# A graph layer on one core: rows turned in the table's loop, words read in the selection, and one run in 12 fetched by SyncE

## The chip, the cores and the metric

The kernel runs on one core of one Trainium2 chip. A core has TensorE (PE), VectorE (DVE), ScalarE (ACT), GpSimd (POOL) and SyncE (SP); each works through its own instructions in their order, and semaphores tie them together. SP computes nothing here: it only issues transfers. The metric is the time of one execution on the device in microseconds. The kernel before takes 3628.49 us (the median of three runs, 3622.15 to 3631.22).

## The reference

A graph has N = 12500 nodes of 128 floats (32 scalars and 32 vectors of three) and E = 412500 edges, sorted by the node that they point to. Cut to what matters:

```python
f0, f1 = x0 @ W1_0e, einsum(x1, W1_1o)          # node features; one half goes along the edges, one stays
e0, e1 = feat0[edge_src], feat1[edge_src]       # one row of 128 floats gathered for every edge
h = gelu(gelu(edge_scalar_attr @ W_mlp1) @ W_mlp2)
w00, w01, w10, w11 = h @ Wp_00, h @ Wp_01, h @ Wp_10, h @ Wp_11     # 4 x 32 weights of an edge
mid = products of w.. with e0, e1 and the edge's four attributes
n0, n1 = segment_sum(mid0, edge_dst), segment_sum(mid1, edge_dst)
y = cos(pi/8) * self + sin(pi/8) * (n @ W2)
out = layernorm(x + y)
```

## The kernel before

**Runs and chunks.** The edges are cut into 806 runs of 512 (four columns q = 0..3 of 128 edges), and four runs make a chunk `c`. For each run `s` a tile `G[s]` (128 partitions, 4 columns, 128 floats) receives the feature row of every edge's source node. There are `LEAD` = 19 such tiles, so run s + 19 takes the tile of run s.

**Four ways to fill a column of G.** All features are first computed into a `table` in device memory.
- POOL gathers a column with an indirect DMA (`gather`, L220), one for each 128 edges. This is the usual way.
- DVE and ACT fill one column of some runs from `xT`, the node matrix kept turned in SBUF: they load node numbers into registers (L176), copy one column of `xT` for each edge (`pick`, L188 and L190), and PE and ACT turn the 128 copies into rows of G (`picked_rows`, L196 and L197). 184 runs get column 2 and 157 runs get column 1 in this way.
- SP fills column 3 of the runs in `aided`, from run 36 on one run in `AID` = 14: 55 runs. `aid(s, t)` loads 16 row numbers into registers (L203) and issues 16 transfers of one row of 512 bytes (L207); eight such groups make a column. The groups of run a are spread over the 12 iterations from a - 16: at the iterations a - 16, -15, -13, -12, -10, -9, -7 and -6. POOL leaves out the columns filled otherwise.
- The first 18 runs (`raw_runs`) are gathered before the table exists: POOL gathers their rows from the input x, PE transposes them (`turn_rows`, L569), ACT copies them to a tile `xt` (L571), PE multiplies by the weights (`features`, L577), and ACT writes the result to a tile `ft` (L579), which then stands for `G[s]`.

**The two loops.** Order on PE, ACT, DVE and SP is the order of the program text (`manual_schedule`); POOL has little but gathers. The table's loop (L875 to L887, iterations b = 0 to 26) loads blocks of 512 nodes, turns them into `xT`, multiplies, and stores the features; small jobs stand at given b (`extra`). The main loop (L907 on) has one iteration for each run s. In it PE makes the edge weights of the coming runs (`weights`, L560), sums the messages of run s - 1 (`segments`, L631 and L633), and DVE makes the messages of run s (`messages`, L602 and twice L606) from the weights in PSUM and from G, with groups of picks in between. `select(c + 1)`, at the end of a chunk, makes the selection matrices of the next chunk (L587 and L595).

**What stands in SP's queue.** In each iteration's order: the edge scalars of four chunks on (`load_edges`, one in four iterations, L487), now and then indices and attributes (L471, L504), the groups of `aid`, and, in `normalise`, the stores of finished nodes (L257), which wait until DVE and ACT have normalised them. A tile is given out again when all its readers are done; an instruction that has to wait for more semaphores than it holds gets instructions ahead of it in the queue that only wait (EVENT_SEMAPHORE).

Of the kernel before, what the change touches and what calls it, by code (L numbers as in the profile page):

```python
# [8 lines left out]
F32 = mybir.dt.float32  # L9
# [12 lines left out]
P = 128  # L22
# [3 lines left out]
Q = 4  # L26
SB = P * Q
J = 8
CH = 4
# [12 lines left out]
LEAD = 19  # L42
RAW = 18
MARGIN = 64
ACC = 768
AID = 14
ROWS = 16
AID_FROM = 36
AID_LEAD = 16
# [2 lines left out]
COL_Q = {DVE: Q - 2, ACT: Q - 3}  # L52
COL_FROM = {DVE: 12, ACT: 16}
LNB = 2


@with_exitstack
def gnn_kernel(ctx: ExitStack, tc: tile.TileContext, x, src, dst, ea4, ea8, w1_0, w1_1, wm1, wm2,
# [8 lines left out]
    nc = tc.nc  # L67
# [55 lines left out]
    for e in SLOTS:  # L123
        picked[e] = []
        while True:
# [3 lines left out]
                break  # L129
            picked[e].append(at + 2)  # L130
    pick_of = {(e, s): i for e, g in picked.items() for i, s in enumerate(g)}
    assert AID_FROM >= raw_runs and AID_LEAD < LEAD and P % ROWS == 0 and STEPS <= AID
    assert all(raw_runs <= g[0] and 0 < len(g) <= 3 * P for g in picked.values())
    assert 0 < len(aided) <= P
# [430 lines left out]
    def turn_rows(s):  # L565

        pt = ps.tile([P, Q, P], F32, name="h")
        for q in range(Q):
            nc.tensor.transpose(pt[:, q, :], G[s][:, q, :], ident)  # L569
        XR[s] = wk.tile([P, Q, P], F32, name="xt", bufs=3)  # L570
        nc.scalar.activation(XR[s], pt, AF.Copy)  # L571

    def features(s):

        pf = ps.tile([P, Q, P], F32, name="h")
        for q in range(Q):
            nc.tensor.matmul(pf[:, q, :], XR[s][:, q, :], wf, start=True, stop=True)  # L577
        G[s] = wk.tile([P, Q, P], F32, name="ft", bufs=3)
        nc.scalar.activation(G[s], pf, AF.Copy)  # L579

    def select(c):


        n = min(CH, NS - c * CH)
        b, r = divmod(c * CH, P)
        oh = wk.tile([P, CH, Q, J], F32, name="oh", bufs=1)
        nc.vector.tensor_tensor(oh[:, :n], iota[:, None, None, :J].to_broadcast([P, n, Q, J]),  # L587
                                rel[b][:, :, r:r + n].rearrange("p q s -> p s q")[:, :, :, None]
                                .to_broadcast([P, n, Q, J]), op=OP.is_equal)
        hot = oh[:, :n].rearrange("p s q j -> p (s q) j")  # L590
        t0 = c * CH % ET * Q
        a = e4[c * CH // ET][:, :, t0:t0 + n * Q].rearrange("p k t -> p t k")
        S_own[c] = owns[c % 2]
        to = S_own[c].rearrange("p t (k j) -> p t k j", j=WIDE)[:, :n * Q, :4, :J]
        nc.vector.tensor_tensor(to, hot[:, :, None, :].to_broadcast([P, n * Q, 4, J]),  # L595
                                a[:, :, :, None].to_broadcast([P, n * Q, 4, J]), op=OP.mult)
# [259 lines left out]
    with tc.manual_schedule(engines={PE, ACT, DVE, SP}):  # L856
        load_raw_rows(nc.sync, 0, min(3, raw_runs))
        load_w1(nc.scalar)
        if raw_runs > 3:
            load_raw_rows(nc.scalar, 3, raw_runs)  # L860
        for s in range(min(LEAD - 2, raw_runs)):
            gather(s)
        nc.vector.tensor_scalar(ident, diag, 0.0, None, op0=OP.is_equal)
        for b in range(min(3, NG)):
            XT[b] = load_nodes(b)
        make_wf()
        clear()
        loads = list(weight_loads())
        new_sums()
        extra = {2: lambda: load_edges(0), 3: lambda: load_attributes(0), NG // 2 - 2: lambda: turn_attributes(0), 4: lambda: load_raws(0), NG // 2: lambda: load_indices(0),  # L870
                 NG // 2 + 3: make_w1b, NG // 2 + 5: make_ws, NG - 6: lambda: radial(0), NG - 4: lambda: mlp1(0),
                 NG - 2: lambda: mlp2(0), NG - 1: make_wpost,
                 NG // 2 + 1: lambda: nc.vector.memset(A["next"], 0.0),
                 NG - 3: tile_places}
        for b in range(NG + 2):  # L875
            if b < NG:
                turn(b)
            if 0 < b <= NG:
                features_of(b - 1)
            if 1 < b:  # L880
                store_nodes(nc.scalar, table, b - 2, PF[b - 2])
            if b + 3 < NG:
                XT[b + 3] = load_nodes(b + 3)
            if b > 4 and loads:
                nc.sync.dma_start(*loads.pop(0))
            if b in extra:
                extra[b]()  # L887
        assert not loads
        for c in range(1, min(EDGES_AHEAD, NCH)):
            load_edges(c)  # L890
        if aided:
            aid_load()
        for s in range(min(LEAD - 2, raw_runs), min(LEAD - 1, NS)):
            gather(s)
        if NCH > 1:
            radial(1)
            mlp1(1)
            mlp2(1)
        weights(0, range(Q))
        select(0)  # L900
        for s in range(min(2, raw_runs)):
            turn_rows(s)
            features(s)
        A["now"] = A["next"]
        clearing = []
        pick_nodes(ACT, 0, 0)
        for s in range(NCH * CH + CH):  # L907
            c, k = divmod(s, CH)
            if s + LEAD - 1 < NS:
                gather(s + LEAD - 1)  # L910
            if k == 3 and c + EDGES_AHEAD < NCH:
                load_edges(c + EDGES_AHEAD)
            if s % P == P // 2 - 16 and (s // P + 1) * P < NS:
                load_raws(s // P + 1)
            if s % P == P // 2 and (s // P + 1) * P < NS:
                load_indices(s // P + 1)
            if s % ET == 8 and s - 8 + ET < NS:
                load_attributes(s // ET + 1)
            for t in range(P // ROWS):
                a = s + AID_LEAD - t * STEPS // (P // ROWS)  # L920
                if a in aided:
                    aid(a, t)
            end = c == NCH - 1
            if k % 2 == 0:
                pick(ACT, len(picking[ACT]) // 2)
            if k % 2 == 0 and s + 2 < NS:
                weights(s + 2, range(Q // 2))
            if k % 2 == 1 and s + 1 < NS:
                weights(s + 1, range(Q // 2, Q))
            if 0 < s <= NS:  # L930
                segments(s - 1)
            if k == 0 and c < NCH:
                places(c)
            if k == 0 and c + 2 < NCH:
                radial(c + 2)
            if s % ET == 21 and s - 21 + ET < NS:
                turn_attributes(s // ET + 1)
            for e in picked:
                if (e, s + 2) in pick_of:
                    picked_rows(e, pick_of[e, s + 2])  # L940
            if k > 1 and c + 2 < NCH:
                pick(ACT, P)
                (mlp1 if k == 2 else mlp2)(c + 2)
                if k == 3 and c + 3 == NCH:
                    nc.scalar.activation(spent, ones, AF.Sqrt)
            pick(ACT, P)
            pick_nodes(ACT, s + 1, 0)
            if s + 2 < raw_runs:
                turn_rows(s + 2)
            if s < NS:  # L950
                for part in range(3):
                    messages(s, part)
                    pick_nodes(DVE, s, part)
                    pick(DVE, P)
            if s + 2 < raw_runs:
                features(s + 2)
            if k == (1 if end else 2) and 0 < c <= NCH:
                add(c - 1)
            if k == 1 and clearing and c < NCH:
                clear_sums(clearing.pop(0)[1])  # L960
            if k < 3 and s < NS:
                pick_nodes(DVE, s, 3)
                pick(DVE, P)
            if k == 1 and 1 < c < NCH:
                norm_on(due.get(c - 2, []))
            if k == 2 and 1 < c < NCH:
                norm_end(due.get(c - 2, []))
            if k == 0 and c == NCH:
                norm_on(due.get(c - 2, []))
                norm_end(due.get(c - 2, []))  # L970
            if c == NCH and k == 1:
                norm_last(due[c - 1])
            if k == (1 if end else 3) and 0 < c < NCH:
                norm(due.get(c - 1, []))
                clearing += [(c, a) for a in range(4)] if c - 1 in due and c < NCH else []
            if k == 3 and c + 1 < NCH:
                select(c + 1)
            if k == 3 and s < NS:
                pick_nodes(DVE, s, 3)
                pick(DVE, P)  # L980
            if s == 1:
                addresses()
                find_first()
                new_sums()
                clearing = [(0, a) for a in range(4)]
            if s == NS - 8:
                count_odd()
# [31 lines left out]
```

## Time and profile before

| | |
|---|---|
| median of three runs | 3628.49 us |
| the profiled execution, its own time | 3639.84 us |
| its span, first to last instruction | 3637.6 us |
| granted TensorE clock, mean | 0.932 |
| busy: PE, DVE, POOL, ACT | 3236.3, 3069.3, 2690.1, 2598.0 us |
| POOL's gathers from the table | 2755 |
| SP's single-row transfers | 7040 |
| messages of the first and last run start at | 102.9 and 3616.9 us |

A row of a group names the line, the engine, the operation and the tiles written and read, then how often it came and how long it took. An engine's name with a q behind it (SPq, DVEq) is its queue: instructions there are not counted as busy time, so SP has no row among the engines. A row of waits says which queue or engine stood at which line until what had ended, with the sum in us, the number of times and the longest. In a row of windows each engine has its busy time and, in brackets, its instructions.

### The profile page before, as it was taken

The page shows a single profiled execution, that of the slowest core. Times are in us where ns is not written, and L with a number is a line of the kernel's source. Part 1 is how long each engine was busy: PE and PEld are TensorE (multiplying, and loading weights), DVE is VectorE, ACT ScalarE, POOL GpSimd, SP SyncE. Part 2 cuts the span into 40 slices and gives each one's busy share as a digit, 9 for nine tenths or more (in the row PEclk, how much of TensorE's full clock was granted, in tenths as well). Part 3 has the DMA queues.
Part 4 walks back from the last instruction along what each step waited for, and adds up shares of the span by engine and source line. Part 5 has one row for each costly group of instructions (what it writes and reads, how often), then busy time and mean ns, then how long its engine had stood idle before and what let it go on. Part 6 is the DMA issues. An engine that isn't in the chain of part 4 may idle for free.

```text
span 3637.6 us, 139391 instructions
## 1 busy us (share of the span) xinstructions
PE 3236.3 (89%) x28542; PEld 2792.6 (77%) x28542; DVE 3069.3 (84%) x27134; ACT 2598.0 (71%) x21720; POOL 2690.1 (74%) x2833
## 2 busy tenths in 40 slices
PE   5899899999889999899889899899989889889998
PEld 4677777787777777777778777788777777777777
DVE  4388888888888888888888888888888888888886
ACT  2377777777777777677767777677777777777785
POOL 7667777777777777777777777777777777777773
PEclk8999998989899999799989999989989999999999
DMA  8223323223322323322223332232232323232231
GB/s 205 54 51 70 63 59 68 63 59 74 63 59 61 69 60 68 68 59 62 65 62 64 70 64 62 58 69 63 65 69 63 61 67 63 62 68 60 63 66 30
DMA packets 579923, 240.84 MB, mean 66 GB/s; under 512 B 484075, under 2 KB 529014, under 8 KB 579078
## 3 DMA queue, kind: packets, MB, share of 16 engines
q0 software_dynamic: 90464, 185.45, 20.0%
q1 hardware_dynamic: 467844, 39.94, 9.0%
q10 hardware_dynamic: 20770, 6.47, 0.8%
q8 instruction: 252, 4.13, 0.5%
q14 instruction: 593, 4.86, 0.4%
HBM read 218.82 MB, written 12.80 MB: 64 GB/s over the span
## 4 chain that ended last, share of the span: by engine, by line
DVE 46%; PE 13%; issue 11%; ACT 7%; DVEq 7%; SPq 7%; POOL 5%; DMA 4%; ACTq 0%; POOLq 0%
DVE gt L188 25%; DVE M L606 13%; DVEq L176 7%; SPq L207 5%; POOL G L220 5%; ACT gt L190 5%; PE sums L631 3%; PE sums L633 3%; DVE own L595 2%; DMA G<-table,idx 2%; DVE M L602 2%; PE w L560 2%; DVE acc L646 2%; PE h L665 2%; SPq L203 1%
## 5 line engine op out<-in xcount | busy, mean ns | idle before, releaser
L220 POOL DMA_INDIRECT G<-table,idx x2755 | 2620.8, 951 | 869.4 <-issue 743.1
L190 ACT ACTIVATE gt<-xT 128x1 f32 x20096 | 1972.2, 189 | 246.1 <-issue 244.4
L188 DVE COPY gt<-xT 128x1 f32 x23552 | 1709.3, 145 | 315.2 <-issue 287.1
L631 PE MATMUL sums<-own,M 128*128 128x96 f32 x6446 | 1348.8, 292 | 5.8 <-DVE M L606 5.5
L633 PE MATMUL sums<-own,M 128*128 128x96 f32 x6446 | 1307.0, 286 | 43.7 <-DVE M L606 43.5
L631 PEld LDWEIGHTS sums<-own,M 128*128 128x128 f32 x6446 | 1039.4, 201 | 101.2 <-DVE M L606 20.5
L633 PEld LDWEIGHTS sums<-own,M 128*128 128x128 f32 x6446 | 1030.0, 201 | 59.6 <-DVE M L606 58.8
L606 DVE TENSOR_TENSOR M<-w,G 128x384 f32<-128x384 f32 x1576 | 861.8, 547 | 0.2
L560 PE MATMUL w<-wpb,h 64*128 64x128 f32 x6448 | 698.3, 308 | 118.4 <-DVE M L606 117.6
L560 PEld LDWEIGHTS w<-wpb,h 64*128 64x128 f32 x6448 | 528.0, 199 | 277.4 <-DVE M L606 150.5
L602 DVE TENSOR_TENSOR M<-w,G 128x256 f32<-128x256 f32 x788 | 328.5, 417 | 35.8 <-PE w L560 8.9
L527 PE MATMUL h<-eT,w1b 64*128 64x128 f32 x3232 | 296.2, 311 | 64.1 <-ACT G L197 54.0
L527 PEld LDWEIGHTS h<-eT,w1b 64*128 64x128 f32 x3232 | 244.6, 209 | 97.2 <-ACT G L197 63.1
L542 PE MATMUL h<-h,w2b 64*64 64x256 f32 x3232 | 282.6, 409 | 31.8 <-ACT h L531 26.4
L197 ACT ACTIVATE G<-h 128x128 f32<-128x128 f32 x341 | 91.2, 272 | 289.7 <-PE h L196 244.2
L531 ACT ACTIVATE h<-h 128x512 f32<-128x512 f32 x404 | 216.0, 585 | 82.0 <-PE h L527 78.4
L547 ACT ACTIVATE h<-h 128x512 f32<-128x512 f32 x404 | 214.3, 580 | 35.5 <-PE h L542 29.6
L542 PEld LDWEIGHTS h<-h,w2b 64*64 64x64 f32 x3232 | 128.6, 138 | 113.4 <-ACT h L531 41.4
L196 PE MATMUL h<-wf,gt 128*128 128x128 f32 x682 | 143.2, 300 | 9.1 <-ACT h L531 5.1
L595 DVE TENSOR_TENSOR own<-oh,e 128x512 f32<-128x512 f32 x202 | 139.8, 692 | 7.1
L646 DVE TENSOR_TENSOR acc<-sums,acc 128x384 f32 x202 | 111.2, 551 | 19.4 <-issue 14.2
L520 ACT ACTIVATE eT<-h 128x128 f32<-128x128 f32 x202 | 53.9, 267 | 97.8 <-PE h L518 77.7
(112 smaller groups left out, 1294.1 us busy)
## 6 DMA issues: line engine op xcount, KB each, us to landing
G<-table SPq DMA_DIRECT2D x7040, 0.5 KB
G<-table,idx POOLq DMA_INDIRECT x2755
e<-in_edge_attr SPq DMA_DIRECT2D x201, 64.0 KB
xt<-in_x SPq DMA_DIRECT2D x24, 256.0 KB
table<-ft ACTq DMA_DIRECT2D x24, 256.0 KB
xt<-in_edge_attr SPq DMA_DIRECT2D x24, 256.0 KB
out<-y SPq DMA_DIRECT2D x24, 256.0 KB
xt<-in_dst SPq DMA_DIRECT2D x5, 256.0 KB
```

Source lines behind the costliest of these rows:

```text
L176: _, r = nc.values_load_multi_w_load_instructions(pick_rows[e, i][:, r0:r1], engines=[e], min_val=x_at, max_val=x_at + 4 * (N - 1), skip_r ...
L188: nc.vector.tensor_copy(to, col)
L190: nc.scalar.activation(to, col, AF.Copy)
L220: nc.gpsimd.indirect_dma_start(out=G[s][:, q, :], out_offset=None, in_=x if s < raw_runs else table, in_offset=bass.IndirectOffsetOnAxis(a ...
L527: nc.tensor.matmul(p1[h][:, j // 2, j % 2, :], w1b[rows, j, :], eT[c][rows, :], start=True, stop=True)
L531: nc.scalar.activation(H1[c][h], p1[h].rearrange("p k j e -> p (k j e)"), AF.Gelu_apprx_tanh, scale=1.0 / math.sqrt(RAD))
L542: nc.tensor.matmul(p2[r][k * HID:(k + 1) * HID, h * n:(h + 1) * n], w2b[rows, :], H1[c][h][rows, k * n:(k + 1) * n], start=True, stop=True)
L560: nc.tensor.matmul(WP[i][:, q, :], H2[c][q % 2][rows, k, q // 2, :], wpb[rows, :], start=True, stop=True)
L602: nc.vector.tensor_tensor(M[s][:, :, :, :MUL], w[:, :, :2 * MUL].rearrange("p q (a u) -> p q a u", a=2), g[:, :, None, :MUL].to_broadcast( ...
L606: nc.vector.tensor_tensor(M[s][:, :, j, MUL:].rearrange("p q (i u) -> p q i u", i=3), w[:, :, None, (2 + j) * MUL:(3 + j) * MUL].to_broadc ...
L631: nc.tensor.matmul(flat[:, bass.ds(at, 4 * FIRST_HALF)].bitcast(F32), M[s][:, q, 0, :], own[:, 3 * WIDE:], start=False, stop=False)
L633: nc.tensor.matmul(sb[:, 1:, bass.ds(at, 4 * WIDE)].bitcast(F32), M[s][:, q, 1, :], own[:, :3 * WIDE].rearrange("p (a j) -> p a j", a=3), ...
```

## The change

Three things are done at once.

- `AID` goes from 14 to 12: the runs whose column 3 comes from SP are 36, 48, ..., 804, which are 65 in place of 55. SP issues 8320 rows in place of 7040; POOL makes 10 gathers fewer. The iterations at which the eight groups of one run are issued, counted from the run, stay as they are.
- `turn_rows` and `features` of the first 14 runs move from the main loop (and from the place just ahead of it) into the table's loop: run i is turned at iteration `TURN_AT[i]` and multiplied one iteration later. The turned rows go into a tile of the ring `M`, and the features are written back into `G[s]`; the tiles `xt` and `ft` are no longer used for this. Runs 14 to 17 stay in the main loop at iterations 12 to 15.
- `select(c)` gets small copies on DVE between L587 and L595, for chunks 10 to 199: one word of each gathered column of the last two runs of that chunk, and one word of each row that SP fetched for an aided run of that chunk. They go into a tile `SEEN` that nothing reads. A copy waits until the transfers that fill what it reads have landed; each engine's queue remembers which counts it has seen.

```diff
-AID = 14
+AID = 12
+TURN_AT = (5, 7, 9, 11, 12, 14, 15, 16, 17, 18, 20, 21, 23, 24)
...
     def turn_rows(s):
...
-        XR[s] = wk.tile([P, Q, P], F32, name="xt", bufs=3)
+        XR[s] = wk.tile([P, Q, 2, P], F32, name="M", bufs=3)[:, :, 0, :]
         nc.scalar.activation(XR[s], pt, AF.Copy)
...
     def features(s):
...
-        G[s] = wk.tile([P, Q, P], F32, name="ft", bufs=3)
+        XR.pop(s)
         nc.scalar.activation(G[s], pf, AF.Copy)
+
+    SEEN = cst.tile([P, 4 * Q], F32)
+    seen_at = [0]
+
+    def read(rows):
+
+        i = seen_at[0] % (4 * Q)
+        seen_at[0] += Q
+        nc.vector.tensor_copy(SEEN[:, i:i + rows.shape[1]], rows)
+
+    def seen(s):
+
+        got = [q for q in range(Q) if not (q == Q - 1 and s in aided or any(q == COL_Q[e] and (e, s) in pick_of for e in picked))]
+        while got:
+            step = got[1] - got[0] if len(got) > 1 else 1
+            n = 1
+            while n < len(got) and got[n] == got[0] + n * step:
+                n += 1
+            read(G[s][:, got[0]:got[n - 1] + 1:step, 0])
+            got = got[n:]
...
     def select(c):
...
         hot = oh[:, :n].rearrange("p s q j -> p (s q) j")
+        if raw_runs <= c * CH - LEAD and (c + 2) * CH < NS:
+            for s in range((c + 1) * CH - 1, (c + 1) * CH - 3, -1):
+                seen(s)
+            for s in range(c * CH, (c + 1) * CH):
+                if s in aided:
+                    read(G[s][:, Q - 1:, 0])
...
             if b in extra:
                 extra[b]()
+            if XR:
+                features(next(iter(XR)))
+            if b in TURN_AT:
+                turn_rows(TURN_AT.index(b))
...
         select(0)
-        for s in range(min(2, raw_runs)):
-            turn_rows(s)
-            features(s)
+        if XR:
+            features(next(iter(XR)))
+        early = len(TURN_AT)
...
-            if s + 2 < raw_runs:
+            if early <= s + 2 < raw_runs:
                 turn_rows(s + 2)
...
-            if s + 2 < raw_runs:
+            if early <= s + 2 < raw_runs:
                 features(s + 2)
```

More of the change, by code (lines that the diff above doesn't have):

```diff
@@ L131, in gnn_kernel @@
     pick_of = {(e, s): i for e, g in picked.items() for i, s in enumerate(g)}
+    assert len(TURN_AT) <= raw_runs <= LEAD - 1 and TURN_AT[-1] < NG + 2
     assert AID_FROM >= raw_runs and AID_LEAD < LEAD and P % ROWS == 0 and STEPS <= AID
```

## The prediction

> **What bounds the kernel now.** First the page: the span, the busy shares, and the groups of POOL and DVE.
>
> ```profile
> span 3637.6 us, 139391 instructions
> PE 3236.3 (89%) x28542; PEld 2792.6 (77%) x28542; DVE 3069.3 (84%) x27134; ACT 2598.0 (71%) x21720; POOL 2690.1 (74%) x2833
> ...
> L220 POOL DMA_INDIRECT G<-table,idx x2755 | 2620.8, 951 | 869.4 <-issue 743.1
> ...
> L188 DVE COPY gt<-xT 128x1 f32 x23552 | 1709.3, 145 | 315.2 <-issue 287.1
> ```
>
> No engine is full by its share. POOL's 74% deceives, though: its idle time is "issue", a fixed pause behind each gather. The view of windows gives its real pace (header, then a stretch in the middle), and the source views of the gather and of the messages (L602, L606) say how far it is ahead.
>
> ```profile
> core 0: us, PE busy (x) PEld busy (x) DVE busy (x) ACT busy (x) POOL busy (x), PEclk, DMA share, GB/s
> 2000.00:3000.00 1000.00, 895.99 (x7945) 774.04 (x7942) 871.22 (x7840) 742.54 (x6287) 756.95 (x798) 0.94 0.30 65
> ...
> L220 POOL DMA_INDIRECT G<-table,idx x2755: 938/944/1467, 94.3 to 3583.3; - x197
> ...
> L602 DVEq EVENT_SEMAPHORE  x1894: 21/50/1855, 109.2 to 3615.1; - x190
> L602 DVE TENSOR_TENSOR M<-w,G x788: 351/415/426, 203.6 to 3616.9; 128x256 f32<-128x256 f32 x197
> L602 DVE TENSOR_TENSOR M<-w,ft x18: 401/425/426, 102.9 to 199.6; 128x256 f32<-128x256 f32 x18
> ...
> L606 DVE TENSOR_TENSOR M<-w,G x1576: 535/547/558, 204.7 to 3617.7; 128x384 f32<-128x384 f32 x197
> ```
>
> 798 gathers in 1000 us are 1.253 us each, so 2755 take 3452 us: POOL has no pause to give away. The messages go at (3616.9 - 203.6) / 787 = 4.34 us for a run, and the last gather starts 33.6 us, or 7 to 8 runs, ahead of the last message. So PE and DVE, in their written order, set the pace, with POOL close behind.
>
> The third queue is in no row of busy time. SP's source views (L207, L203), and two pieces of its timeline:
>
> ```profile
> L207 SPq MOVE G<-table x7040: 29/29/103, 155.2 to 3561.8; - x196
> L207 SPq DMA_DIRECT2D G<-table x7040: 227/228/544, 196.5 to 3561.9; - x196
> ...
> L203 SPq TENSOR_LOAD <-aid_at x440: 1160/1262/1804, 153.7 to 3555.2; - x147
> ```
> ```profile
> 1925.44 18.66 SPq L207 DMA_DIRECT2D G<-table  x48
> 1944.20 0.41 SPq L487 DMA_DIRECT2D e<-in_edge_attr  x1
> 1946.06 18.26 SPq L207 DMA_DIRECT2D G<-table  x48
> ...
> 2038.15 5.11 SPq L207 DMA_DIRECT2D G<-table  x16
> 2061.54 1.95 SPq L257 DMA_DIRECT2D out<-y  x2
> ```
>
> Three groups of 16 rows and one transfer of edge scalars take 1946.06 - 1925.44 = 20.62 us with no pause between them. Only ahead of the stores at 2061.54 does SP stand still, for some 18 us. How much it stands still in all, from its first row to its last, is in the view of SP's waits for 196 to 3563 us:
>
> ```profile
> SPq L257 <- ACT y L704: 191.9, 21, 21.4
> SPq L207 <- DVE M L606: 57.6, 18, 8.7
> SPq L207 <- PE h L569: 41.2, 1, 41.2
> SPq L257 <- ACT G L197: 20.8, 2, 19.6
> SPq L207 <- DMA xt<-in_src: 3.6, 2, 3.2
> ```
>
> The 41.2 us end with the first row. In the 3365 us from 196.5 to 3561.9 SP therefore waits some 270 us (191.9 + 57.6 + 20.8), 8%, for stores and for free G tiles, and works 3095 us. This 8% is all that it can take on.
>
> **The change part by part.**
>
> *AID from 14 to 12.* SP gets 10 runs more, each 8 loads of row numbers and 128 rows. What a run costs, in two ways. From the timeline: 20.62 us less 0.5 for the edge scalars (0.41 and its wait) over three groups is 6.71 us, times 8 is 53.7 us. From the stage: 3095 us less all else in SP's queue, over 55. All else is, by its source views (L487, L257, L504),
>
> ```profile
> L487 SPq DMA_DIRECT2D e<-in_edge_attr x202: 368/405/2088, 11.9 to 3562.8; - x101
> ...
> L257 SPq DMA_DIRECT2D out<-y x25: 384/411/889, 334.1 to 3632.8; - x25
> ...
> L504 SPq DMA_DIRECT2D xt<-in_edge_attr x25: 347/372/1779, 136.8 to 3505.6; - x25
> ```
>
> 227 transfers at 0.5 us with the wait beside each, and L504 with a dozen loads of indices at 0.45: 130 us. That leaves 2965 / 55 = 53.9 us. SP's work becomes 65 x 53.7 + 130 = 3620 to 65 x 53.9 + 130 = 3634 us; I take 3625. The stage began with 3365 us, waits and all, so SP no longer fits: 12 runs at 4.34 us are 52.1 us, and in them SP has one aided run and three edge transfers, 53.9 + 1.5 = 55.4 us. It falls behind by over 3 us in 12 runs; its waits vanish first, then DVE waits for it. Behind the late rows in SP's queue stand the edge scalars (PE's `radial` waits), the stores, and indices.
>
> How late may SP be? The last group of run a is issued at iteration a - 6; the new copy in `select` asks for it at a - 1 (36 and 12 are multiples of 4, so an aided run opens its chunk). Edge scalars loaded at iteration 4c + 3 are used at 4c + 8. So after five iterations, some 22 us, the other engines go at SP's pace of 55.4 / 12 = 4.62 us a run.
>
> The Trainium skill, DMA: Bandwidth & Descriptors, section "Issuing engines are not separate DMA queues", says that issuing from another engine only saves sequencer time, "which is usually small relative to the DMA itself". By that rule ten more fetched runs would cost SP next to nothing, and the second case below would be the result (3551 us instead of 3828). The trace does not agree here: for a row of 512 bytes the issue, 228 ns and a move beside it, is what fills SP.
>
> POOL loses 10 gathers, 12.5 us by 1.253 us; hidden, since POOL is then not the last.
>
> *Words read in the selection.* Per chunk about three copies of a few words, and one more in a third of the chunks; the nearest row is L188's copy of one word, 0.145 us: 0.5 us a chunk, 0.12 us a run, with a few waits of 50 ns. In return the waits ahead of L602 go (1894 x 50 ns = 95 us, 0.12 us a run) and some of the 287.1 us that L188 stands idle behind them. The bounds of the net are a loss of 0.12 and a gain of 0.12 + 287.1 / 788 = 0.48 us a run; I take a gain of 0.1, because two waits in the queue are the usual and only the pause behind them can shrink. The copies ask for gathers four runs early; POOL is 7 to 18 runs ahead, so they hold nothing up: `own` (L595), the picks and PE's `segments` stand behind them. As long as SP is last, all of this is cover work and worth nothing.
>
> *Fourteen runs turned in the table's loop.* What a turned run costs PE, and what room there is (page groups, then windows of the first 100 us with the columns above):
>
> ```profile
> L577 PE MATMUL h<-wf,xt 128*128 128x128 f32 x144 | 20.8, 288 | 13.8 <-ACT xt L571 13.8
> L569 PE MATMUL h<-ident,G 128*128 128x128 f32 x72 | 11.8, 288 | 5.5 <-ACT h L547 2.8 <-ACT h L531 2.7
> ```
> ```profile
> 0.00:50.00 50.00, 29.72 (x187) 27.92 (x188) 21.35 (x34) 10.73 (x17) 35.61 (x44) 0.86 0.97 221
> 50.00:100.00 50.00, 26.30 (x207) 21.84 (x205) 16.36 (x44) 11.80 (x21) 37.40 (x39) 0.80 0.69 164
> ```
>
> 32.6 us for 18 runs is 1.8 us of PE each, 25 us for 14; PE has 44 us idle there and ACT 77. The loop waits for transfers (DMA share 0.97), which hides most of it; if a gather is later than its iteration, PE stands in its order and the table ends later. The bounds for the main loop's start are 4 us earlier (the two turns ahead of it are gone) and 25 us later. I take 100 us in place of 102.9 for the first message, nearest to the idle rows.
>
> In the main loop 18 runs took (199.6 - 102.9) / 17 = 5.69 us each. Twelve iterations lose their turn and then go at 4.34 at most: 12 x 1.35 = 16 us less. The messages of run 17, whose tile SP's first aided run (36) takes, then end at 199.6 + 2 - 2.9 - 16, about 182, or 178 if runs without picks go faster: 180 us.
>
> *The sum.* SP starts its rows at 180 us and works 3625 us; a few early waits for stores, while it is not yet late, are 5 (0 to 20). Its last row, now of run 804, goes out at 3810. From there: landing 2 us (in the chain of waits a gather's pieces are of that size,
>
> ```profile
> 2969.72 2.35 DMA G<-table,idx
> ```
>
> the last of the long ones), the messages of runs 804 and 805 some 5, and from the last message (3617.7) to the span's end (3637.6) 20 us. Span 3837. The profiled execution took 3639.84 for a span of 3637.6, so 3839; the median of the runs shown (3628.49) stands 11 us below that execution: 3828 us, 5.5% slower.
>
> **The rivals.** *SP is not last, POOL is* (faster). For: SP's waits leave it 8%, and DVE and POOL are both relieved. Against: the arithmetic of SP's row, whose 228 ns hardly vary (227 at least). It decides if an aided run costs SP under about 50 us. Then POOL starts run 19 at about 102, needs 2741 x 1.253 = 3434 us, and 24 us follow: span 3560, median 3551. This is where the skill's rule would lead.
>
> *SP keeps pace, and the copies change nothing* (they do not remove the waits, since other counts remain). Then 180 + 788 x 4.34 + 20 = 3620, median about 3611.
>
> *SP's waits stay beside the added work* (slower still). If the stores go on holding SP up 213 us (191.9 + 20.8) because the other engines fall behind together with it: 3828 + 213, some 4040. Against it: a store at iteration i waits for normalising at i, and late SP comes there five iterations after the others.
>
> **How the numbers follow.** SP last: 0.84. POOL last: 0.06. Pace kept: 0.04. Waits stay: 0.06. The time is that of the first, 3828. Its range: low with SP at 3620 and starting at 165 (runs without picks at 4 us), no early waits, and rows at the quicker piece's 18.26 in place of 18.66 for part of them, 3775; high with a table's loop that gives all 25 us back (start at 200), 3634, waits of 20 and the profiled execution's own offset, 3885. The others lie outside with 0.16 together. About 0.3% is what a measurement of this kernel can tell from no change: faster 0.09, same 0.02, slower 0.89.
>
> **What would show it.** Right: SP's rows from about 180 to beyond 3780 us with the waits at L257 nearly gone; messages at 4.6 us a run; DVE idle at the new copies until the transfer from the table lands; POOL waiting for free G tiles all through; PE under 88%. The first messages at 100 and run 17 near 180 show the third part. The waits ahead of L602 should fall well below 1894. Wrong: SP's timeline with pauses left, or a group under 6.3 us; or a table's loop whose last store goes out much later than now (its row, from the source view of L257: 90.4 us), which would shift everything after it.
>
> ```profile
> L257 ACTq DMA_DIRECT2D table<-ft x25: 357/378/433, 12.8 to 90.4; - x25
> ```

## The result and the profile after

| | before | after |
|---|---|---|
| time, median of 4 runs | 3628.76 us | 3831.64 us |
| lowest to highest | 3622.15 to 3631.22 | 3829.41 to 3832.94 |
| ratio (95% interval) | | 1.0556 (1.0541 to 1.0571) |
| profiled execution, its span | 3639.84, 3637.6 | 3830.36, 3828.6 |

The profiled execution of before is not one of its four runs. The change makes the kernel 5.6% slower. The lines of the page that answer to those shown of before are the span, the busy shares and the chain that ended last:

```profile
span 3828.6 us, 142163 instructions
PE 3296.3 (86%) x28542; PEld 2866.6 (75%) x28542; DVE 3080.8 (80%) x27709; ACT 2599.9 (68%) x21720; POOL 2679.8 (70%) x2823
...
SPq 55%; issue 14%; DVE 11%; PE 10%; ACT 4%; DMA 3%; DVEq 1%; POOL 1%; ACTq 0%; POOLq 0%
SPq L209 40%; SPq L205 12%; DVE gt L190 5%; ACT gt L192 3%; DVE M L634 3%; PE sums L659 2%; PE sums L661 2%; PE w L562 2%; SPq L489 1%; DVEq L178 1%; POOL G L222 1%; PE h L529 1%; DVE M L630 1%; DMA e<-in_edge_attr 1%; DMA G<-table 1%
```

Before, the first line of the same chain was

```profile
DVE 46%; PE 13%; issue 11%; ACT 7%; DVEq 7%; SPq 7%; POOL 5%; DMA 4%; ACTq 0%; POOLq 0%
```

The share of every engine has fallen, and no engine is the bound. SP's queue, 7% of the chain before, is now 55% of it: the rows (L209, before L207) and the loads of their numbers (L205, before L203). The line numbers have moved by the new lines: the gather is L222, the messages L630 and L634, the edge scalars L489, the stores L259, and the new copies are L590.

The source views of the changed kernel give the pace. A row has the line, the operation and its count, its duration in ns (min/median/max), and the starts of the first and the last.

```profile
L209 SPq DMA_DIRECT2D G<-table x8320: 227/228/406, 172.0 to 3806.1; - x199
L205 SPq TENSOR_LOAD <-aid_at x520: 1142/1271/2091, 134.8 to 3799.9; - x174
...
L222 POOL DMA_INDIRECT G<-table,idx x2745: 938/944/1566, 103.0 to 3727.2; - x197
...
L630 DVE TENSOR_TENSOR M<-w,G x806: 354/414/425, 108.7 to 3808.9; 128x256 f32<-128x256 f32 x162
L630 DVEq EVENT_SEMAPHORE  x550: 21/21/11844, 96.6 to 3807.8; - x184
...
L590 DVEq EVENT_SEMAPHORE  x860: 21/21/2290, 263.5 to 3767.5; - x172
L590 DVE COPY SEEN<-G x575: 138/160/419, 263.7 to 3767.8; 128x4 f32<-128x4 f32 x74, 128x1 f32<-128x1 f32 x70, 128x2 f32<-128x2 f32 x48
```

SP's rows go out from 172.0 to 3806.1 us, 3634 us, and the last message starts 2.8 us behind the last row. POOL starts its last gather 82 us ahead of the last message; before, it was 34 us. The messages of runs 18 to 805 take (3808.9 - 172.0) / 788 = 4.62 us each, where they took 4.34.

A piece of SP's timeline, and SP's waits from its first row to its last (in all 21 us, of which these are the largest):

```profile
1920.61 18.66 SPq L209 DMA_DIRECT2D G<-table  x48
1939.37 0.41 SPq L489 DMA_DIRECT2D e<-in_edge_attr  x1
1941.25 18.23 SPq L209 DMA_DIRECT2D G<-table  x48
```
```profile
SPq L259 <- ACT G L199: 6.9, 1, 6.9
SPq L209 <- DMA xt<-in_src: 3.2, 1, 3.2
SPq L489 <- PE sums L661: 1.9, 5, 0.5
```

Three groups and one transfer of edge scalars still take 1941.25 - 1920.61 = 20.64 us. What is gone is the standing still: 289 us before (270 in the three largest waits, which the prediction added up, and 19 in small ones), 21 now, with not one long wait for a store. SP's work is thus 3634 - 21 = 3613 us.

Who waits for SP stands in the view of all waits:

```profile
DVE SEEN L590 <- DMA G<-table: 342.7, 56, 13.5
...
PE h L520 <- DMA e<-in_edge_attr: 244.2, 75, 8.5
...
DVE gt L190 <- issue: 125.4, 453, 1.1
...
POOL G L222 <- DMA G<-table: 80.8, 31, 11.7
...
POOL G L222 <- DVE M L634: 77.7, 108, 4.1
```

DVE stands 343 us at the new copies until SP's rows have landed, PE 244 us at the edge scalars that come behind the rows in SP's queue, and POOL waits 159 us, 81 for SP's rows and 78 for messages that free a tile. The place itself, in DVE's timeline (the bracket is the idle time just before, and what ended it):

```profile
2010.20 0.23 DVE L590 COPY SEEN<-G 128x4 f32<-128x4 f32 x2
2015.92 0.15 DVE L590 COPY SEEN<-G 128x1 f32<-128x1 f32 x1 [5.49 <-DMA G<-table]
2015.99 0.68 DVE L623 TENSOR_TENSOR own<-oh,e 128x512 f32<-128x512 f32 x1
```

Two copies of gathered words pass at once, the copy of the word that SP fetched waits 5.5 us, and `own` with all that follows it stands behind.

One more number has moved: the granted TensorE clock was 0.894 in this execution, 0.932 before, and PE is busy for 3296 us in place of 3236. Whether that could be the cause is taken up below.

### The profile page after: what moved, and what is told of

Its sections match the earlier page's. It is cut to its first block, busy times and chain, and to the rows that moved or that the text cites. A ratio compares the mean times of both kernels' runs of the same rounds, so it can differ in the third digit from the quotient of the medians.

```text
span 3828.6 us, 142163 instructions
## 1 busy us (share of the span) xinstructions
PE 3296.3 (86%) x28542; PEld 2866.6 (75%) x28542; DVE 3080.8 (80%) x27709; ACT 2599.9 (68%) x21720; POOL 2679.8 (70%) x2823
## 4 chain that ended last, share of the span: by engine, by line
SPq 55%; issue 14%; DVE 11%; PE 10%; ACT 4%; DMA 3%; DVEq 1%; POOL 1%; ACTq 0%; POOLq 0%
SPq L209 40%; SPq L205 12%; DVE gt L190 5%; ACT gt L192 3%; DVE M L634 3%; PE sums L659 2%; PE sums L661 2%; PE w L562 2%; SPq L489 1%; DVEq L178 1%; POOL G L222 1%; PE h L529 1%; DVE M L630 1%; DMA e<-in_edge_attr 1%; DMA G<-table 1%
## 5 line engine op out<-in xcount | busy, mean ns | idle before, releaser
L222 POOL DMA_INDIRECT G<-table,idx x2745 | 2610.9, 951 | 1023.2 <-issue 784.2
L659 PE MATMUL sums<-own,M 128*128 128x96 f32 x6446 | 1387.3, 300 | 6.6 <-DVE M L634 6.3
L661 PE MATMUL sums<-own,M 128*128 128x96 f32 x6446 | 1344.0, 293 | 14.6 <-DVE M L634 13.9
L659 PEld LDWEIGHTS sums<-own,M 128*128 128x128 f32 x6446 | 1089.1, 209 | 93.7 <-issue 12.3
L661 PEld LDWEIGHTS sums<-own,M 128*128 128x128 f32 x6446 | 1073.0, 209 | 21.0 <-DVE M L634 19.7
L634 DVE TENSOR_TENSOR M<-w,G 128x384 f32<-128x384 f32 x1612 | 880.6, 547 | 0.3
L562 PE MATMUL w<-wpb,h 64*128 64x128 f32 x6448 | 674.4, 316 | 37.3 <-DVE M L634 36.1
L562 PEld LDWEIGHTS w<-wpb,h 64*128 64x128 f32 x6448 | 519.4, 208 | 183.4 <-issue 91.1
L630 DVE TENSOR_TENSOR M<-w,G 128x256 f32<-128x256 f32 x806 | 333.9, 414 | 56.2 <-PE w L562 16.8
L590 DVE COPY SEEN<-G 128x4 f32<-128x4 f32 (+2 forms) x575 | 67.2, 177 | 343.3 <-DMA G<-table 342.7
L544 PE MATMUL h<-h,w2b 64*64 64x256 f32 x3232 | 295.7, 417 | 35.3 <-ACT h L533 28.8
L520 PE MATMUL h<-ident,e 128*128 128x128 f32 x202 | 63.8, 316 | 248.5 <-DMA e<-in_edge_attr 244.2
L520 PEld LDWEIGHTS h<-ident,e 128*128 128x128 f32 x202 | 33.9, 168 | 260.2 <-issue 234.6
```

Of the source, the lines that this page charges most:

```text
L222: nc.gpsimd.indirect_dma_start(out=G[s][:, q, :], out_offset=None, in_=x if s < raw_runs else table, in_offset=bass.IndirectOffsetOnAxis(a ...
L544: nc.tensor.matmul(p2[r][k * HID:(k + 1) * HID, h * n:(h + 1) * n], w2b[rows, :], H1[c][h][rows, k * n:(k + 1) * n], start=True, stop=True)
L562: nc.tensor.matmul(WP[i][:, q, :], H2[c][q % 2][rows, k, q // 2, :], wpb[rows, :], start=True, stop=True)
L630: nc.vector.tensor_tensor(M[s][:, :, :, :MUL], w[:, :, :2 * MUL].rearrange("p q (a u) -> p q a u", a=2), g[:, :, None, :MUL].to_broadcast( ...
L634: nc.vector.tensor_tensor(M[s][:, :, j, MUL:].rearrange("p q (i u) -> p q i u", i=3), w[:, :, None, (2 + j) * MUL:(3 + j) * MUL].to_broadc ...
L659: nc.tensor.matmul(flat[:, bass.ds(at, 4 * FIRST_HALF)].bitcast(F32), M[s][:, q, 0, :], own[:, 3 * WIDE:], start=False, stop=False)
```

## The experiments

The theory: SP's queue has become the last to end, because ten more aided runs fill its pauses and more, and neither of the other two parts costs anything that shows. The main rival: the copies hold DVE up by waiting early, so that the slowdown is theirs and stays when AID goes back. Two more are that the added transfers cost by their traffic, and that PE is slower by its clock. A further question is how far the time follows SP's occupancy alone.

Two sets (the first four runs told below, and the four under the split) were made on chips on which every kernel, the one before too, took about 5510 us at a granted clock of 0.74. Ratios there compare only with the kernel before on the same chip.

**The first set: 5510 us chips.** Four kernels. The first is the changed kernel with AID set back:

```diff
-AID = 12
+AID = 14
```

> The changed kernel with one aided run in 14 again, all else as changed. Theory (SyncE's queue is full at one in 12): SyncE has 55 x 53.9 + 130 = 3095 us of work from 172 us on, so it is not last and its waits at the stores come back. Then GpSimd is last: its first gather from the table starts at 103 us, 2755 x 1.253 = 3452 us follow, then 24 us: about 3580 us, and the copies wait for gathers. If GpSimd is not last either, the 788 runs go at 4.24 us from 172 us on: about 3535. Rival (the copies in the selection hold DVE up by themselves, since they ask for whole chunks early): the time stays at 3800 or more, because the copies are still there.

The second is the kernel before with only AID changed to 12:

```diff
-AID = 14
+AID = 12
```

> The kernel before with one aided run in 12 as its only edit. Theory: SyncE's rows start at 196 us as before and take 65 x 53.9 + 130 = 3634 us, then 24 us: about 3855 us, slower than the whole change by the 24 us that the earlier start of the rows saves there. The waits for late rows stand at the messages (L602) and not at copies. Rival (the copies are the cause): about 3620, a little under the kernel before, since GpSimd has 10 gathers fewer.

The third is the changed kernel, still with 12, with twice the rows in a group (half as many loads of numbers, the same 8320 transfers; the four groups of run a then stand at the iterations a - 16, -13, -10 and -7):

```diff
-ROWS = 16
+ROWS = 32
```

> The changed kernel with 32 row numbers in one load of SyncE's registers in place of 16: as many rows, half the loads. Theory: a load of 32 takes about 1.9 us (16 take 1.27), so an aided run costs SyncE 4 x (32 x 0.332 + 1.9) = 50 us in place of 53.9, 65 x 50 + 130 = 3380 us from 172 us on: it ends at 3552, level with GpSimd (103 + 2745 x 1.253 = 3543). With the 24 us behind it the time is about 3575, between 3560 and 3620, and the 256 us are gone although all 8320 rows are still copied. Rival (the added row transfers themselves are what costs, by their traffic or because they land late): the time stays within 50 us of 3832.

The fourth is the changed kernel one step back:

```diff
-AID = 12
+AID = 13
```

> The changed kernel with one aided run in 13: 60 of them, half of the added rows. Theory: the cost has a threshold, not a slope. SyncE needs 53.9 + 1.6 = 55.5 us for 13 runs, 4.27 us a run, just under the 4.37 that GpSimd's gathers take; it works 60 x 53.9 + 130 = 3364 us from 172 us on, ends at 3536, and GpSimd is last: 103 + 2750 x 1.253 + 24 = 3573 us. Rival (each aided run more costs its share): half way between the changed kernel and the one with 14, about 3705.

Against 5509.79 us for the kernel before: AID back at 14 took 5542.79 (1.006, 1.0041 to 1.008), only AID 12 took 5557.81 (1.0095, 1.0068 to 1.0123), groups of 32 took 5523.75 (1.0027, 1.0007 to 1.0048), AID 13 took 5519.97 (1.0018, 0.9989 to 1.0047). The expected times were for chips like that of the profile, and these runs can't be held against them: in the first kernel PE is busy for 4150 us here (3235 where the same kernel takes 3600 us, told below), and every engine is idle for a larger share of the time. In the view of waits of the first kernel DVE stands before its picks, with nothing in the profile that it waits for, eight times as long as above:

```profile
DVE gt L190 <- issue: 977.9, 1798, 1.3
```

SP is slowed too: the rows of the second kernel go out from 292.9 to 5532.1 us, which, less 123 us of waits and the 130 us of other transfers, is some 77 us for each of 65 runs in place of 54. In kind the second kernel agrees with the theory. Its SP has no wait for a store left, where the first kernel's has 192 us of them (153.6 and 38.3); it is 48 us slower than before; and DVE waits for SP's rows at the messages, since it has no copies at which to wait:

```profile
DVE M L602 <- DMA G<-table: 118.4, 24, 10.7
```

In size these chips decide nothing about 3830 us, and the first kernel's 33 us more than before (0.6%) had the sign that the rival wants. So the first and the third were run again elsewhere.

**AID back to 14, groups of 32: the same two kernels at 3630 us.** On another chip, where the kernel before took 3631.29 us.

> The changed kernel with one aided run in 14 again, on a chip where the kernel before takes about 3630 us (a first look fell on one where every kernel took about 5500). Theory (SyncE's queue is full at one in 12): SyncE has 3095 us of work from 172 us on and is not last; GpSimd is: 103 + 3452 + 24, about 3580 us. If GpSimd is not last either, 3535. Rival (the copies in the selection hold DVE up by themselves): 3800 or more.

Measured: 3599.17 us (3593.65 to 3608.63), ratio 0.9905 (0.9879 to 0.9932). So the changed kernel with 14 is not only back, it is 32 us faster than before, and of all kernels run here the fastest. The rival falls: copies and early turns together cost nothing, and the slowdown is AID's (3831.64 - 3599.17 = 232 us; the kernel before differs by 2.5 us between the two chips). Its source views, the largest of SP's waits, and the row of the copies:

```profile
L222 POOL DMA_INDIRECT G<-table,idx x2755: 943/947/1493, 105.1 to 3577.6; - x197
...
L630 DVE TENSOR_TENSOR M<-w,G x806: 353/415/426, 111.0 to 3585.7; 128x256 f32<-128x256 f32 x162
```
```profile
SPq L259 <- ACT y L732: 193.0, 21, 24.6
```
```profile
DVE gt L190 <- issue: 125.9, 452, 0.9
...
DVE SEEN L590 <- DMA G<-table,idx: 84.8, 63, 3.5
```

SP stands 193 us at the stores again (283 in all from its first row to its last), so it has room. The last gather now starts 8 us ahead of the last message, where it was 34 us before, and the gathers go at (3577.6 - 105.1) / 2754 = 1.261 us each without a gap, so POOL can't end earlier. It isn't alone: the chain that ended last runs through DVE for 31%, PE for 15% and POOL for 15%, so the three are about level. The copies now wait for POOL's gathers. Of the 31 us by which the last message comes earlier (3616.9 to 3585.7), 25 are POOL's lead used up, and only 8 are left of it. The time missed the 3580 us expected by 19, most of it in POOL's pace: expected were a first gather at 103, 1.253 us for each and 24 us behind the last; measured were 105.1, 1.261 (20 us more in all) and 28.9. The median stands 9 us below the profiled execution, which gives a part back.

> The changed kernel with 32 row numbers in one load in place of 16, on a chip where the kernel before takes about 3630 us. Theory: an aided run costs SyncE about 50 us in place of 53.9, it ends at 3552, level with GpSimd, and the time is about 3575 (3560 to 3620), though all 8320 rows are still copied. Rival (the added transfers themselves cost, by their traffic or by landing late): within 50 us of 3832.

Measured: 3720.7 us (3719.59 to 3722.36), ratio 1.0246 (1.0194 to 1.0299). Both expectations missed: it is neither back at 3575 nor unmoved. Source views, and waits:

```profile
L209 SPq DMA_DIRECT2D G<-table x8320: 227/228/520, 173.6 to 3699.2; - x199
...
L205 SPq TENSOR_LOAD <-aid_at x260: 2040/2192/3054, 135.8 to 3686.9; - x130
```
```profile
SPq L259 <- ACT G L199: 11.9, 3, 11.2
```
```profile
DVE SEEN L590 <- DMA G<-table: 57.6, 34, 5.5
```

SP sends the same 8320 rows in 3525.6 us where it took 3634.1: 108.5 us less, and the time is 111 us less. SP still has hardly a wait (25 us in all from its first row to its last), so it is still last, and the time follows its occupancy nearly one to one. With the traffic unchanged, it is the instructions on SP that count and not the bytes. My estimate put SP's end at 3552, 147 us too early. About half of that is the load: one of 32 numbers takes 2.19 us, not the 1.9 I had taken, 75 us over 260 loads. 25 are the waits, which it left out; the rest, some 45 us, I haven't traced.

The clock as the cause falls too. PE is busy for 3296 us with AID 12 and for 3235 with 14, at granted clocks of 0.894 and 0.922: 61 us of work more can't make 232 us of time, and PE has idle time enough to take them (244 us before the edge scalars alone). SP's rows, which do fill the time, have kept their 228 ns.

**The split on 5510 us chips.** AID 13 and only AID 12 again, beside two kernels that each keep one of the other two parts with AID at 14: the copies alone (early turns undone), and the turns alone:

```diff
-        if raw_runs <= c * CH - LEAD and (c + 2) * CH < NS:
+        if False:
```

> The changed kernel with one aided run in 13: 60 of them, half of the added rows. Theory: the cost has a threshold, not a slope. SyncE needs about 3400 us from 172 us on and ends near 3570, beside GpSimd (last gather 5 x 1.26 = 6 us earlier than the 3577.6 us with one in 14), so the time is close to that with one in 14 (3599): about 3593, between 3580 and 3615. Rival (each aided run more costs its share): half way to 3832, about 3715.

> The kernel before with one aided run in 12 as its only edit. Theory: SyncE's rows start at 196 us as before and take the 3634 us that they took in the changed kernel, then 22 us: about 3852 us, 20 more than the whole change, and the waits for late rows stand at the messages. Rival (the copies are needed for the loss): about 3620.

> The kernel before with the copies in the selection as its only edit (one aided run in 14, turning where it was). Theory: GpSimd is close behind in the kernel before (last gather at 3583 us, 33.6 us ahead of its use), so the copies can give at most that lead: DVE's idle time behind the waits falls by half, GpSimd's last gather stays at 3583 us, 29 us follow, a span of 3612, about 3605. Rival (the copies cost as much as they give): 3629, unchanged.

> The kernel before with 14 runs turned in the table's loop as its only edit (no copies, one aided run in 14). Theory: run 17 is done at 172 us in place of 200, the pace after it stays 4.34 us a run: 28 us earlier, 3600, unless GpSimd (first gather from the table at 105 us, 2755 x 1.26, 29 us: 3605) holds it at about 3605. Rival (the gain at the start is given back to GpSimd, whose first gather from the table starts 10 us later): 3625 or more.

The chip was again one of those at 5510 us (5512.91 for the kernel before). AID 13: 5528.41 (1.0018, 0.9991 to 1.0045). Only AID 12: 5554.72 (1.008, 1.0052 to 1.0107). Copies only: 5536.75 (1.0029, 0.9992 to 1.0065). Turns only: 5522.21 (1.0017, 0.9996 to 1.0038). Only the second stands off from 1, and its waits for SP's rows are again there:

```profile
DVE M L602 <- DMA G<-table: 203.4, 32, 15.1
```

How the 32 us of the kernel with 14 divide between copies and turns at 3630 us is therefore not settled, nor what AID 12 alone costs there. That it costs time without the copies, at the messages, two chips show.

**Where SP's queue is full.** AID 13 gives SP 60 aided runs in place of 55 or 65, and POOL 5 gathers less than with 14. The first try also gave ACT more picks, to take gathers off POOL:

```diff
-AID = 12
+AID = 13
...
-SLOTS = {DVE: [(8, 8, 8, 0), (8, 8, 8, 8), (8, 8, 8, 8), (8, 8, 8, 8)], ACT: [(24,), (28,), (24,), (28,), (24,)]}
+SLOTS = {DVE: [(8, 8, 8, 0), (8, 8, 8, 8), (8, 8, 8, 8), (8, 8, 8, 8)], ACT: [(28,)]}
```

> The changed kernel with one aided run in 13 and 28 picks for ACT in every run (24 or 28 before), which takes some 15 columns from GpSimd. Theory (threshold): 60 aided runs are 60 x 53.1 + 150 = 3340 us of work for SyncE from 173 us on, which ends near 3515 if it never waits, so it is not last; GpSimd makes about 20 gathers fewer than with one aided run in 14 and 24 or 28 picks, 20 x 1.26 = 25 us of 3577.6: last gather 3552, 29 us behind it, about 3580, between 3565 and 3605. Rival (slope: every aided run more costs its share of 233 us): 3715 less what GpSimd saves, 3690 or more. On a chip where the kernel before takes about 5500 us neither can be told.

Measured: 3685.89 us (3668.65 to 3696.32) against 3631.05, ratio 1.0129 (1.0086 to 1.0172; the quotient of the two medians is 1.0151). That misses the 3580, but it isn't SP either: SP still stands at its stores.

```profile
SPq L259 <- ACT y L732: 113.1, 20, 18.2
```
```profile
PEld h L544 <- ACT h L533: 113.0, 169, 3.9
...
PE h L529 <- ACT G L199: 100.6, 49, 3.7
```

The next kernel has AID 13 alone:

> The changed kernel with one aided run in 13 as its only edit, the picks of ACT as they were. It tells apart two readings of the run with 13 and 28 picks (3686 us). If the picks of ACT made that loss (theory: SyncE needs some 3330 us of work for 60 aided runs, 4.23 us a run, and keeps up with 4.34), the time is near that with one in 14: about 3595, between 3580 and 3625, with waits of over 100 us at SyncE's stores. If one in 13 makes it (each aided run more costs its share, or the rows are late by the order of SyncE's queue), it stays at 3670 or more, up to the slope's 3715.

Measured: 3620.71 us (3614.61 to 3629.42) against 3634.46, ratio 0.9967 (0.9947 to 0.9987). It fell within the expected 3580 to 3625, 26 us above the 3595 named. Its source view of the rows, SP's waits, and its waits at the same places:

```profile
L209 SPq DMA_DIRECT2D G<-table x7680: 227/228/345, 174.8 to 3579.0; - x197
```
```profile
SPq L259 <- ACT y L732: 27.9, 17, 7.2
...
SPq L259 <- ACT G L199: 14.6, 2, 13.4
```
```profile
DVE SEEN L590 <- DMA G<-table: 120.6, 27, 11.8
...
PE h L529 <- ACT G L199: 59.2, 51, 3.0
...
PEld h L544 <- ACT h L533: 39.0, 73, 3.5
```

So ACT's extra picks cost the kernel before this one 65 us (3685.89 - 3620.71): PE waits longer for ACT's edge network (113 us in place of 39, 101 in place of 59). The 65 us are measured, with one edit between the two; that they pass through PE's waits is read from the views and not tested apart. And SP at one run in 13 has 42.5 us of its waits for stores left, where the expectation named over 100 as a sign: it is nearer to full than I had thought. SP's share of the chain that ended last says the same: 6% with 14, 24% with 13, 55% with 12. From 14 to 13 the five runs more cost 22 us, from 13 to 12 the next five cost 211. By 53.6 us a run these are 268 us of work; 43 fill the last waits (64 us in all with 13, 21 with 12), and the remaining 225 are close to the 211 seen.

## Why the prediction was right

The forecast was 3828 us with SP's queue last, and the measured time is 3831.64. Step by step:

- **An aided run costs SP 53.7 to 53.9 us.** Four kernels give it now: the time from first row to last, less all waits in it, less the 130 us of other transfers, over the runs. The kernel before: (3365 - 289 - 130) / 55 = 53.6; the prediction's 53.9 had left the 19 us of small waits among the work. 55 runs (AID 14): (3357 - 283 - 130) / 55 = 53.5. 60 runs: (3404 - 64 - 130) / 60 = 53.5. 65 runs: (3634 - 21 - 130) / 65 = 53.6. The sum said 3625 of work and 5 of waits, 3630; it was 3613 and 21, 3634. The two terms missed by -12 and +16, and offset each other: 65 x 53.6 + 130 is 3614.
- **The skill's rule.** The Trainium skill, DMA: Bandwidth & Descriptors, section "Issuing engines are not separate DMA queues", holds sequencer time to be usually small beside the transfer. For one row alone this trace is no clear case against it: SP issues 16 rows in 5.11 us, 0.32 each (the piece of before in the prediction), and the last message starts 2.8 us behind the last row, so the landing may well take longer than the issue. What does not hold here is the conclusion that ten more fetched runs then cost next to nothing: SP's work of issuing is 3613 of 3634 us, one issue behind the other, and the case to which the rule led (3551 us) didn't come.
- **SP's waits vanish first, then DVE waits for it.** Right: 289 us became 21, and DVE's wait at the copies is 343. The edge scalars behind the rows were named too (PE, 244 us at `radial`), and the stores no longer wait, so the rival by which they would go on waiting (4040) fell.
- **4.62 us a run.** Measured 4.62, over runs 18 to 805.
- **The first message at 100.** Wrong by 9 us: it came at 108.7, within the bounds that were given (4 us earlier to 25 later). The last store of the table went at 99.7 (before: 90.4). The step that failed is the value between the bounds: I took the idle time of PE and ACT in this loop as room, but the turns stand in a fixed order with the table's blocks. In the changed kernel's timeline:

```profile
71.83 1.06 PE L579 MATMUL h<-wf,M 128*128 128x128 f32 x8
...
83.24 0.38 ACTq L259 DMA_DIRECT2D table<-ft  x1
83.82 0.60 ACT L581 ACTIVATE G<-h 128x512 f32<-128x512 f32 x1 [11.98 <-DMA G<-in_x,idx_raw]
...
101.13 0.28 ACT L522 ACTIVATE eT<-h 128x128 f32<-128x128 f32 x1 [2.75 <-DMA table<-ft]
```

  ACT stood still 12 us ahead of a turned run's copy. The view puts this on a gather of raw rows, but PE had multiplied this run's turned rows at 71.83, so its gathers had landed by then. What held ACT is the table store ahead of the copy in its queue: the trace has the end of the store's wait at 83.19 us, just behind the last landing (83.17) of a transfer of edge scalars that SP issued at 77.56 and that counts on the same semaphore. Before, the corresponding store went at 77.41, so about 6 of the 9 us are there at this place. How much of them the turns make, and how much a later SP, isn't settled. The first edge network (`eT`) then comes behind the last stores, and its weights set the first message.
- **Run 17 done at 180.** It was 172, by SP's first row, which waits for it. The loop began 9 us late, but 18 runs took (172.0 - 108.7) / 18 = 3.5 us each and not the 4.4 of the sum. So two misses partly cancelled: without turns the early runs, which have no picks, go faster than those of the middle, which I had named and put in the range only.
- **The end.** From SP's last row to the span's end 27 us were predicted and 22.5 measured: the landing and two runs' messages come at 2.8 us behind the last row, not at 7.
- **Profiled against median.** I took the median 11 us below the profiled execution, as before. After, it stands 1 us above it (3831.64 against 3830.36): the runs differ little here (3829.41 to 3832.94), and so they do with groups of 32 (3719.59 to 3722.36), the other kernel in which SP sets the time. This error of 12 us is what offsets the 8 us early start and the 4.5 us shorter tail. The agreement of 4 us in the whole is thus better than its terms.
- **The copies.** The waits ahead of the messages fell from 1894 to 550, with 860 of them now at the copies. DVE's pauses before picks fell from 287 to 125 us, against 67 us of copies. As said, none of it counts while SP is last. With AID at 14 the copies, together with the turns, are worth 32 us, and POOL's pace then bounds the gain.
- **POOL.** Waiting for free tiles, as predicted (78 us for the messages, 81 for rows). The kernel that is left without SP's limit takes 3599, with POOL's gathers going without a gap.

## What to carry to other kernels

A queue that only issues transfers has no busy row, but it has an occupancy: count its instructions and their spacing, subtract from the stage, and the rest is all the work that it can take on. Below that line added work is nearly free (22 us for five runs), above it nearly every microsecond shows (211 us for the next five), so a split among engines is set where the helper still has waits. Of the three settings here the best was 14, with 283 us of SP's waits left; 13, with 64, cost 22 us, and 12, with 21, cost 232. When several parts are changed together, set back the one that loads the fullest queue: here the other two were a gain of 0.95% that a loss of 5.6% hid.

## What was not expected of the hardware

- A load of 16 numbers into SP's registers takes 1.27 us (median), one of 32 takes 2.19: by a straight line through the two, 0.057 us for a number more and 0.35 us that don't depend on it. Larger groups saved 108 us of SP's time, but could not bring it below the other engines.
- The chips differ: some took 5510 us for a kernel that others ran in 3630, at a granted clock of 0.74 against 0.93, and with pauses of issue before DVE's picks of 978 us in place of 125. Against the kernel before on the same chip, the kernel with groups of 32 was 2.5% slower at 3630 us and 0.3% at 5510, and the one with AID 14 0.95% faster at 3630 and 0.6% slower at 5510, so a balance between queues that is tuned on one may not hold on the other.
